# The first stage of element 0 computed by nodes instead of by features

## The chip, the core and the metric

The kernel runs on one core of one Trainium2 chip. The metric is device time in microseconds: 2378.89 us, the median of three runs (2378.59 to 2378.9). All data are float32. TensorE is written PE below, VectorE DVE, ScalarE ACT, GpSimd POOL, SyncE SP; SP, ACT and POOL also issue DMAs.

## The reference

Sixteen elements (graphs of 1024 nodes with 128 features, a full 1024 x 1024 adjacency of weights) pass through two blocks, each followed by a residual and a normalization over the features:

```
# block 0 (embeddings = x, both matrices = adj)
degree = adj.sum(-1)[:, :, None]
sum_neighbors = einsum('bid,bij->bjd', x, adj) / degree
x = layernorm(x + relu(concat([x, sum_neighbors], -1) @ W.T + b))

# block 1: four layers on x, with skips of earlier layers' outputs
def layer(nodes, adj, ws, bs, wd, bd, wn, bn, wu, bu):
    src_agg = einsum('bjv,bij->biv', nodes @ ws + bs, l2norm(adj, rows))
    dst_agg = einsum('bjv,bji->biv', nodes @ wd + bd, l2norm(adj, columns))
    return tanh(concat([src_agg, nodes @ wn + bn, dst_agg], 2) @ wu + bu)
x = layernorm(x + four_layers(x))
```

The degree of a node divides all features of its gathered sum, so it may be applied after the product with the second half of W as well as before it. The norms of the rows and the columns of adj need the sums of squares of all its entries.

## The kernel before

The elements are worked one after another. For elements 1 to 15 the whole first block overlaps the last layers of the element before. Element 0 has nothing before it, so its first block is a stretch of its own, written out line by line (L1131 to L1344), and its layer 0 (the branch `if b == 0`) is a "plain layer" with work hung between the products as hooks: the number of a hook is the number of the product ahead of which it runs. Two z products with the own weights come first (steps 0 and 1), then eight d products of half 1 (2 to 9), eight of half 0 (10 to 17), then sixteen z products with the transposed adjacency (18 to 33).

The order of instructions on every engine is the order in which the program writes them (`manual_schedule`); each engine runs its own list in order, and semaphores hold an instruction until its inputs and its buffer are ready. PSUM buffers come from pools that go round: `ps_s`, reached through `small(...)`, has two banks; `ps_t`, reached through `product(...)` without a number, has four. A buffer is taken again when everything that reads its last contents has run. Each DMA takes one of eight completion semaphores in turn and waits for the DMA that had it before.

The first block of element 0, in order:

- SP (and POOL) load the nodes xn and the adjacency a, in four pairs of row blocks (`PAIRS`, the upper half of the nodes first). Then SP loads layer 0's and layer 1's weights and the bias vectors (`load_biases`), layer 2's weights, adjacency row quarter 2, layer 3's weights, quarters 3, 0 and 1 (`load_rows`). The quarters are loaded once more by rows because they are scaled by the inverse row norms and transposed into `at`.
- `to_xT`: PE transposes the nodes, ACT copies them to xT (features by nodes).
- `squares_of`, `gathers_of`: ACT squares each row block with a row sum (L1225), DVE sums degrees (L1231), PE accumulates the gathered sums pa (L1238). POOL adds the blocks of squares (`add_square`, L1228) for the column norms; ACT's square of the last block, `second`, comes late.
- `degree_inverses` and `degree_row`: the reciprocal degrees, one number per node and so one per partition, are turned by PE into rows that repeat over all partitions (`factor_bank`, L361), copied by ACT into dinv (L1258). `scaled` multiplies the gathered sums by them (L1261) into agT.
- `weights_of_x`, `weights_of_agT`: PE multiplies by the two halves of W (L1265, L1268), features by nodes; ACT applies bias and relu (L1269).
- `with_x`: PE transposes the result back to nodes by features (L1276), DVE adds x (L1278).
- `norm_stats` (L491 to L521): batch statistics per block on DVE; POOL raises the variance to -1/2 with one instruction for the half (L518). `norm_write` on DVE or `norm_write_act` on ACT normalizes in place; `to_x1` transposes to x1T.
- Between these, `fold_begin` and `fold_end` turn each layer's weights into products with wu: PE transposes (L207) into banks, copies by ACT (L208), bias products (L211, L213), weight products (L229), copies (L231, L232).

In layer 0: `messages` forms the messages t from x1T (PE L249, DVE L740), four groups with `second_x1`, `factors_and_fold` and `row_factors0` behind the first three. There `row_inverses` spreads the inverse row norms (DVE L403), `gather_inverses` makes rinv, `column_transpose` and `column_reduce` sum the squares by columns (DVE L341, L346), and `scale_rows` scales row quarters by rinv on ACT, eight instructions a quarter (L688). In the plain layer: hook 2 ends the column inverses on POOL (L397), hook 6 makes the rows cinv of them (PE L361 cinvp, ACT L353), hook 3 transposes quarters 2 and 3 on DVE (L696), `columns0` scales the columns of a in place (L436), `destination` multiplies a half of d by cinv (L904), hooks 9 and 12 fold layer 3's weights, with the scalings of quarters 0 and 1 at hooks 9 and 14, `sums0` combines quarters of the matrices for the next layer (L715, L719, L721) and `finish` adds z and leads to the tanh (L907, L1107). The layer after starts with its messages, tile pt from f1T (L249).

Of the kernel before, what the change touches and what calls it, by code (L numbers as in the profile page):

```python
# [8 lines left out]
F32 = mybir.dt.float32  # L9
# [14 lines left out]
def adj_resnorm_kernel(ctx: ExitStack, tc: tile.TileContext, x, adj, w0, b0, layers, out):  # L24
# [1132 lines left out]
    biases_of = [[b0, *layers[0][1::2], *layers[1][1::2]], [*layers[2][1::2], *layers[3][1::2]]]  # L1157
# [3 lines left out]
    bcs = [columns[0][:, 1:5], columns[0][:, 5:], columns[1][:, :4], columns[1][:, 4:]]  # L1161

    def load_biases(i, q, s=slice(None)):
        for k, v in list(enumerate(biases_of[i]))[s]:
            q.dma_start(in_rows[k:k + 1, i * P:(i + 1) * P], v.rearrange("(o p) -> o p", o=1))

# [84 lines left out]
    yT = one.tile([P, N], F32, tag="f23T", name="yT0")  # L1251
    x1n = two.tile([P, NB, D], F32, tag="sq", name="x1n0")
    x1T = one.tile([P, N], F32, tag="xb", name="x1_0_T")
    dinv = one.tile([P, N], F32, tag="acc", name="dinv0")
    pn, pw = {}, {}

    def degree_row(h):
        nc.scalar.copy(nodes(dinv[:, half(h)]), blocks(factor_bank(2, h, inv, f"dinv0_{h}")))  # L1258

    def scaled(h):  # L1260
        nc.vector.tensor_mul(agT[:, half(h)], pa[h], dinv[:, half(h)])  # L1261

    def weights_of_x(h):
        pw[h] = product(f"pw0_0_{h}")
        nc.tensor.matmul(pw[h], w0T[:, 0], xT[:, half(h)], start=True, stop=False)  # L1265

    def weights_of_agT(h):
        nc.tensor.matmul(pw[h], w0T[:, 1], agT[:, half(h)], start=False, stop=True)  # L1268
        nc.scalar.activation(blocks(yT[:, half(h)]), nodes(pw[h]), AF.Relu, bias=b0c)  # L1269

    def with_x(h):

        pt = ps_t.tile([P, BPH, P], F32, tag="pt", name=f"yn0_{h}")
        for q in range(BPH):
            i = h * BPH + q
            nc.tensor.transpose(pt[:, q], yT[:, i * P:(i + 1) * P], ident)  # L1276
        pn[h] = x1n[:, h * BPH:(h + 1) * BPH]
        nc.vector.tensor_add(pn[h], pt, xn[:, h * BPH:(h + 1) * BPH])  # L1278
# [7 lines left out]
    weights_of_x(1)  # L1286
# [9 lines left out]
    degree_row(1)  # L1296
# [3 lines left out]
    add_square(1)  # L1300
# [510 lines left out]
```

## Time and profile before

The profiled execution took 2377.85 us; its span, from the first to the last instruction, is 2375.8 us.

| engine | busy us | share |
|---|---|---|
| PE (matmul) | 2365.3 | 100% |
| PE (weight load, beside it) | 1309.7 | 55% |
| DVE | 2092.3 | 88% |
| ACT | 981.4 | 41% |
| POOL | 282.7 | 12% |

The stretch that the change touches, by the same execution (busy us of each engine, share of the DMA engines):

| us from the start | PE | DVE | ACT | POOL | DMA |
|---|---|---|---|---|---|
| 7 to 18 | 9.22 of 11 | 5.91 | 5.54 | 5.44 | 1.04 |
| 18 to 24 | 5.90 of 6 | 4.17 | 4.19 | 5.48 | 0.62 |
| 24 to 34 | 9.04 of 10 | 6.35 | 6.15 | 4.31 | 0.70 |
| 34 to 48 | 13.89 of 14 | 12.47 | 8.10 | 6.32 | 1.13 |
| 48 to 64 | 16.00 of 16 | 13.58 | 13.79 | 8.06 | 0.90 |
| 64 to 78 | 14.00 of 14 | 13.86 | 0.72 | 1.42 | 0.94 |

How to read it: PE's products are pipelined and the ends of them are modelled, so that a stretch that shows PE as busy throughout can hold small waits. A float32 product of 128 x 512 appears as two passes. In the lists of the timeline a row gives the start, the length, the engine, the line, the operation, the tiles written and read, the number of instructions joined in the row, and in brackets the idle time before it and what ended that. In the chain of waits a row gives the start, the length and what was running. In the list of waits a row gives who waited for whom, the total in us, how many times, and the longest. DMA-issuing instructions on SP show the time that SP took to issue them, not the transfer.

### The profile page before, as it was taken

To read this page: it belongs to the slowest core of one execution; us is meant where nothing else is said; L and a number is where in the kernel's file an instruction comes from. 1 tells how busy PE (TensorE), PEld (TensorE's weight loads), DVE (VectorE), ACT (ScalarE), POOL (GpSimd) and SP (SyncE) were. 2 spreads that over 40 slices of the span, in tenths; PEclk is the share of its full clock that TensorE was granted. 3 is DMA by queue.
4 is the path that set the end of the run, shared out by engine and by line. 5 is a ranking of instruction groups with operands and counts; after the bars stand their busy time and mean duration, and the time that the engine had idled before them with its cause. 6 is when DMAs were issued, how large, how long until landed. Compare 5 with 4: busy or idle time off the path is not lost.

```text
span 2375.8 us, 39260 instructions
## 1 busy us (share of the span) xinstructions
PE 2365.3 (100%) x15259; PEld 1309.7 (55%) x15259; DVE 2092.3 (88%) x2821; ACT 981.4 (41%) x1859; POOL 282.7 (12%) x104
## 2 busy tenths in 40 slices
PE   9999999999999999999999999999999999999998
PEld 5455555555555555555655555555555555555555
DVE  6999998998988989889988889898899998998954
ACT  6425335352443524445243452534425334352322
POOL 5100111101111011111011110111100111101100
PEclk9999999999999999999999999999999999999999
DMA  8536263362624527244273442725426263362410
GB/s 208 127 89 144 57 141 75 80 138 49 159 60 98 116 54 166 51 106 106 64 156 69 104 92 71 153 65 120 87 72 145 58 139 75 78 142 49 100 22 22
DMA packets 363403, 232.03 MB, mean 98 GB/s; under 512 B 150369, under 2 KB 334322, under 8 KB 363218
## 3 DMA queue, kind: packets, MB, share of 16 engines
q1 hardware_dynamic: 360578, 226.18, 42.6%
q0 software_dynamic: 816, 2.49, 0.4%
q8 instruction: 121, 1.98, 0.3%
q10 hardware_dynamic: 1824, 0.85, 0.1%
q14 instruction: 64, 0.52, 0.1%
HBM read 209.59 MB, written 19.84 MB: 97 GB/s over the span
## 4 chain that ended last, share of the span: by engine, by line
PE 99%; DMA 0%; DVE 0%; SPq 0%; issue 0%; ACT 0%; POOLq 0%; POOL 0%; DVEq 0%
PE m L1094 43%; PE z L1094 26%; PE pt L249 9%; PE pt_z L249 5%; PE m_f L624 5%; PE z_f L624 2%; PE pw L249 2%; PE m3s L1094 2%; PE z L913 1%; PE d L913 1%; PE pt_p L249 1%; PE pa L1238 0%; DMA a<-in_adj_dram 0%; PE wm L229 0%; PE wtr L207 0%; PE pw L1268 0%
## 5 line engine op out<-in xcount | busy, mean ns | idle before, releaser
L1094 PE MATMUL m<-a,t 128*64 128x512 f32 x1008 | 426.7, 593 | 0.0
L1094 PE MATMUL m<-at,t 128*64 128x512 f32 x1008 | 420.4, 592 | 0.0
L1094 PE MATMUL m<-T,S 128*64 128x512 f32 (+1 forms) x1040 | 398.6, 572 | 0.0
L1094 PE MATMUL m<-Q,S 128*64 128x512 f32 x880 | 392.3, 592 | 0.0
L484 POOL TENSOR_TENSOR rs<-ve,mhalf 128x32 f32<-128x32 f32 x30 | 192.1, 6403 | 1018.8 <-DVE ve L482 1018.8
L1094 PE MATMUL z<-at,t 128*64 128x512 f32 (+1 forms) x520 | 229.6, 579 | 0.0
L1094 PE MATMUL z<-a,S 128*64 128x512 f32 x504 | 228.3, 592 | 0.0
L1094 PE MATMUL z<-Q,t 128*64 128x512 f32 (+1 forms) x520 | 227.5, 580 | 0.0
L1094 PE MATMUL z<-a,t 128*64 128x512 f32 (+1 forms) x520 | 227.4, 580 | 0.0
L1094 PE MATMUL z<-at,S 128*64 128x512 f32 x504 | 226.6, 592 | 0.0
L1094 PEld LDWEIGHTS m<-Q,S 128*64 128x64 f32 x880 | 119.4, 137 | 187.2 <-issue 186.5
L1094 PEld LDWEIGHTS m<-T,S 128*64 128x64 f32 x1040 | 133.1, 137 | 123.9 <-issue 118.8
L1094 PEld LDWEIGHTS m<-at,t 128*64 128x64 f32 x1008 | 133.5, 137 | 115.0 <-issue 115.0
L1094 PEld LDWEIGHTS m<-a,t 128*64 128x64 f32 x1008 | 131.3, 137 | 98.6 <-issue 93.6
L946 ACT COPY e<-m 64x512 f32<-64x512 f32 x63 | 36.6, 581 | 339.0 <-PE m L1094 338.6
L1094 PE MATMUL z<-T,t 128*64 128x512 f32 (+2 forms) x400 | 173.0, 575 | 0.0
L397 POOL TENSOR_TENSOR inv<-cols,mhalf 128x16 f32<-128x16 f32 (+1 forms) x16 | 50.0, 3124 | 935.3 <-DVE cols L396 935.3
L436 DVE TENSOR_TENSOR a<-a,cinv 128x512 f32<-128x512 f32 x250 | 154.6, 697 | 0.0
L324 ACT ACTIVATE sq<-a 128x1024 f32<-128x1024 f32 x120 | 125.8, 1050 | 33.0 <-DVE acc L331 19.1
L1094 PEld LDWEIGHTS z<-Q,t 128*64 128x64 f32 x520 | 69.6, 137 | 107.2 <-issue 106.8
L249 PEld LDWEIGHTS pt<-wm,f1T 128*64 128x64 f32 x1536 | 111.1, 137 | 27.0 <-issue 14.9
L319 ACT ACTIVATE a<-a 128x1024 f32<-128x1024 f32 x120 | 125.3, 1045 | 0.4
(328 smaller groups left out, 4999.5 us busy)
## 6 DMA issues: line engine op xcount, KB each, us to landing
a<-in_adj_dram SPq DMA_DIRECT2D x120, 512.0 KB
rows<-in_adj_dram SPq DMA_DIRECT2D x480, 64.0 KB
a<-in_adj_dram SPq DMA_DIRECT2D x240, 128.0 KB
wm<-wsave SPq DMA_DIRECT2D x32, 704.0 KB
wm<-wsave SPq DMA_DIRECT2D x31, 320.0 KB
xs<-in_x_dram SPq DMA_DIRECT2D x60, 128.0 KB
cinv<-dr SPq DMA_DIRECT2D x30, 256.0 KB
dinv<-dr SPq DMA_DIRECT2D x30, 256.0 KB
```

What stands on the lines that cost most here:

```text
L249: nc.tensor.matmul(out[s], x[:, s], y, start=start, stop=stop)
L319: nc.scalar.activation(a[:, i, :], a[:, i, :], AF.Copy, accum_out=degree)
L324: nc.scalar.activation(sq, a[:, i, :], AF.Square, accum_out=state["cols"][:, i:i + 1])
L397: nc.gpsimd.tensor_tensor(inv[:, s], cols[:, s], mhalf[:, s], ALU.pow)
L436: engine.tensor_mul(a[:, i, s], a[:, i, s], cinv[:, s])
L484: nc.gpsimd.tensor_tensor(rstd, ve, mhalf[:, :n], ALU.pow)
L624: nc.tensor.matmul(o, x_, y_, start=start, stop=stop)
L913: nc.tensor.matmul(nodes(o) if len(y.shape) == 4 else o, x_, y, start=start, stop=stop)
L946: nc.scalar.copy(e0[high], A[high])
L1094: nc.tensor.matmul(o, x, y_, start=start, stop=stop)
```

## The change

All of it is in element 0.

- The two products with W give nodes by features at once: blocks of xT (and of agT, now the unscaled gathered sums, copied by ACT) are the stationary operand, W the moving one (`into_rows`). The transposes back and the degree rows go. The inverse degree is a scalar of the partition: DVE multiplies the second product by it and adds the first with the bias row b0r (`x_and_bias`, `with_degrees`); relu and the residual are one instruction (`with_x`). b0r is loaded by a DMA that repeats b0 over the partitions.
- The statistics are done by pairs of blocks (`two_stats`), each with a power of its own on POOL.
- The squares of the last two row blocks are made earlier, and two additions of squares go to DVE; one of POOL's goes away.
- Biases are loaded in three groups: of layers 0 and 1 on SP ahead of layer 1's weights, of layer 2 on ACT's queue, of layer 3 on SP behind row quarter 2.
- The spread of the row inverses and rinv come ahead of the messages; two of quarter 2's scalings come into `second_x1`. Quarters 0 and 1 are scaled at hooks 8 and 9, ahead of layer 3's fold (hooks 13 and 16), and transposed at hook 12. POOL takes four of the column scalings of half 0 in place of six.

The diff, cut to its core:

```diff
-    biases_of = [[b0, *layers[0][1::2], *layers[1][1::2]], [*layers[2][1::2], *layers[3][1::2]]]
+    biases_of = [[b0, *layers[0][1::2], *layers[1][1::2]], layers[2][1::2], layers[3][1::2]]
+    b0r = one.tile([P, N], F32, tag="acc", name="b0r")[:, :P]
-        nc.scalar.copy(nodes(xT[:, half(h)]), blocks(pt))
+        nc.scalar.copy(xT[:, half(h)], pt)
     for l, q in enumerate((None, None, 2, 3)):
-        if l in (1, 2):
-            load_biases(l - 1, nc.sync)
+        if l == 3:
+            load_biases(2, nc.sync)
         fetched.append(fetch_weights(raw, l, nc.sync, bcs[l], None if l else wm))
+        if l == 0:
+            nc.sync.dma_start(b0r, b0.rearrange("(o p) -> o p", o=1).to_broadcast([P, P]))
+            load_biases(0, nc.sync)
...
+    def into_rows(name, xs, k, h):
+        pw[k, h] = ps_t.tile([P, BPH, P], F32, tag="pt", name=f"{name}_{h}")
         for q in range(BPH):
             i = h * BPH + q
-            nc.tensor.transpose(pt[:, q], yT[:, i * P:(i + 1) * P], ident)
+            nc.tensor.matmul(pw[k, h][:, q], xs[:, i * P:(i + 1) * P], w0T[:, k], start=True, stop=True)
+    def gathered(h):
+        nc.scalar.copy(blocks(agT[:, half(h)]), nodes(pa[h]))
+    def x_and_bias(h):
+        nc.vector.tensor_add(xw[:, rows_of(h)], pw[0, h], b0r[:, None, :].to_broadcast([P, BPH, P]))
+    def with_degrees(h, qs):
+        for q in qs:
+            i = h * BPH + q
+            nc.vector.scalar_tensor_tensor(xw[:, i], pw[1, h][:, q], inv[:, 2 * NB + i:2 * NB + i + 1], xw[:, i],
+                                           op0=ALU.mult, op1=ALU.add)
+    def with_x(h):
+        s = rows_of(h)
+        nc.vector.scalar_tensor_tensor(x1n[:, s], xw[:, s], 0.0, xn[:, s], op0=ALU.max, op1=ALU.add)
+    def two_stats(h, first, shifted=False):
...
+        for q in (first, first + 1):
+            nc.vector.bn_stats(stats[:, q], x1n[:, h * BPH + q])
+            nc.vector.bn_aggr(mv[:, q], stats[:, q])
+        nc.vector.tensor_scalar_add(ve[:, s], mv[:, s, 1], LN_EPS)
...
+        nc.gpsimd.tensor_tensor(rstd[:, s], ve[:, s], mhalf[:, s], ALU.pow)
...
-    weights_of_x(1)
+    into_rows("px", xT, 0, 1)
...
     degree_inverses(1)
-    degree_row(1)
     squares_of(*PAIRS[2])
     gathers_of(*PAIRS[2])
     add_square(0)
-    add_square(1)
...
     gather(1, second)
+    square(first)
+    degree_inverses(0)
+    x_and_bias(1)
+    gathered(1)
+    into_rows("px", xT, 0, 0)
+    into_rows("pg", agT, 1, 1)
+    square(second)
+    load_biases(1, nc.scalar)
+    nc.vector.tensor_add(sq[1], sq[1], sq[first])
+    add_square(1)
+    x_and_bias(0)
+    gather(0, first)
     bias_columns(0)
-    degree_inverses(0)
-    degree_row(0)
-    scaled(1)
-    weights_of_agT(1)
-    gather(0, first)
-    square(first)
     gather(0, second)
-    add_square(first)
-    scaled(0)
+    gathered(0)
+    with_degrees(1, range(BPH))
     with_x(1)
-    weights_of_x(0)
-    weights_of_agT(0)
-    stats = {1: norm_stats(pn[1], range(BPH), "0_0_1", True)}
-    fold_begin(0, fetched[0])
-    with_x(0)
+    two_stats(1, 0, True)
+    biases = fold_begin(0, fetched[0], later=True)
+    into_rows("pg", agT, 1, 0)
+    two_stats(1, 2)
+    root_inverses(cols, inv, slice(NB))
+    biases()
     fold_end(0, fetched[0])
-    square(second)
-    other_half = norm_stats(pn[0], range(2), "0_0_0", then=True)
-    for q in range(2, BPH):
-        norm_write(pn[1][:, q], pn[1][:, q], stats[1], q)
-    stats[0] = other_half(range(2, BPH))
-    root_inverses(cols, inv, slice(NB))
-    add_square(second)
-    biases = fold_begin(1, fetched[1], nc.vector.tensor_copy, True)
-    for q in range(2):
-        norm_write_act(pn[1][:, q], pn[1][:, q], stats[1], q)
+    with_degrees(0, range(2))
+    written(1, 0, norm_write_act)
+    biases = fold_begin(1, fetched[1], later=True)
+    for q in range(1, BPH):
+        written(1, q)
+    with_degrees(0, range(2, BPH))
+    spread = row_inverses(0, inv)
     to_x1(1)
     biases()
     fold_end(1, fetched[1])
+    with_x(0)
+    two_stats(0, 0)
+    rinv = gather_inverses(0, spread)
+    two_stats(0, 2)
     for q in range(BPH):
-        norm_write(pn[0][:, q], pn[0][:, q], stats[0], q)
+        written(0, q)
...
             def row_factors0():
-                for q in (2, 3):
-                    scale_rows(rows[q], q, rinv)
+                scale_rows(rows[2], 2, rinv, range(2, QB))
+                scale_rows(rows[3], 3, rinv)
             def second_x1():
                 bias_columns(1)
                 fold_begin(2, fetched[2])
-                ahead["spread"] = row_inverses(0, inv)
+                scale_rows(rows[2], 2, rinv, range(2))
+                nc.vector.tensor_add(sq[4], sq[4], sq[second])
                 ahead["tr"] = column_transpose(0, st0)
...
             hooks = {0: weights0, 2: lambda *_: inverses(0, st0, NB), 3: rows0, 6: cinv0,
-                     9: lambda *_: fold_and_scale(3, 0), 11: second0, 12: folded(3, fold_end),
-                     14: lambda *_: scale_rows(rows[1], 1, rinv), 18: first0, 26: sums0}
+                     8: lambda *_: scale_rows(rows[0], 0, rinv), 9: lambda *_: scale_rows(rows[1], 1, rinv),
+                     11: second0, 12: first_rows, 13: fold_last, 16: lambda *_: fold_end(3, fetched[3]),
+                     14: lambda *_: columns0(range(NJ, NB), 0, nc.gpsimd), 18: first0, 26: sums0}
```

`fold_last` is `bias_columns(2)` and `fold_begin(3, ...)`; `first_rows` transposes quarters 0 and 1 and scales the columns 0 to 3 of half 1; `second0` keeps the scaling of columns 4 to 7 of half 1 and `destination(1)`; `first0` is `destination(0)` and DVE's scaling of columns 0 to 3 of half 0.

More of the change, by code (lines that the diff above doesn't have):

```diff
@@ L1160, in adj_resnorm_kernel, with load_biases @@
     columns = [raw.take(len(v)) for v in biases_of]
-    bcs = [columns[0][:, 1:5], columns[0][:, 5:], columns[1][:, :4], columns[1][:, 4:]]
-    def load_biases(i, q, s=slice(None)):
-        for k, v in list(enumerate(biases_of[i]))[s]:
+    bcs = [columns[0][:, 1:5], columns[0][:, 5:], columns[1], columns[2]]
+    def load_biases(i, q):
+        for k, v in enumerate(biases_of[i]):
             q.dma_start(in_rows[k:k + 1, i * P:(i + 1) * P], v.rearrange("(o p) -> o p", o=1))
+    b0r = one.tile([P, N], F32, tag="acc", name="b0r")[:, :P]
     def bias_columns(i):
@@ L1250, in adj_resnorm_kernel @@
     agT = one.tile([P, N], F32, tag="f1T", name="agT0")
-    yT = one.tile([P, N], F32, tag="f23T", name="yT0")
+    xw = one.tile([P, NB, D], F32, tag="f23T", name="xw0")
     x1n = two.tile([P, NB, D], F32, tag="sq", name="x1n0")
     x1T = one.tile([P, N], F32, tag="xb", name="x1_0_T")
[L1254 to L1273, printed above, removed]
+    pw, of_half = {}, {}
+    def rows_of(h):
+        return slice(h * BPH, (h + 1) * BPH)
@@ L1274, in with_x @@
+    def into_rows(name, xs, k, h):
+        pw[k, h] = ps_t.tile([P, BPH, P], F32, tag="pt", name=f"{name}_{h}")
         for q in range(BPH):
             i = h * BPH + q
-            nc.tensor.transpose(pt[:, q], yT[:, i * P:(i + 1) * P], ident)
-        pn[h] = x1n[:, h * BPH:(h + 1) * BPH]
-        nc.vector.tensor_add(pn[h], pt, xn[:, h * BPH:(h + 1) * BPH])
+            nc.tensor.matmul(pw[k, h][:, q], xs[:, i * P:(i + 1) * P], w0T[:, k], start=True, stop=True)
+    def gathered(h):
+        nc.scalar.copy(blocks(agT[:, half(h)]), nodes(pa[h]))
@@ new lines, in two_stats @@
+    def two_stats(h, first, shifted=False):
+        if h not in of_half:
+            of_half[h] = (one.tile([P, BPH, 6], F32, tag="stats", name=f"st0_0_{h}"), [
+                two.tile([P, BPH, n] if n > 1 else [P, BPH], F32, tag=tag, name=f"{tag}0_0_{h}")
+                for tag, n in (("mv", 2), ("ve", 1), ("rst", 1), ("shift", 1))])
+        stats, (mv, ve, rstd, shift) = of_half[h]
+        s = slice(first, first + 2)
+        for q in (first, first + 1):
+            nc.vector.bn_stats(stats[:, q], x1n[:, h * BPH + q])
+            nc.vector.bn_aggr(mv[:, q], stats[:, q])
+        nc.vector.tensor_scalar_add(ve[:, s], mv[:, s, 1], LN_EPS)
+        if shifted:
+            nc.vector.tensor_scalar_mul(shift[:, s], mv[:, s, 0], -1.0)
+        nc.gpsimd.tensor_tensor(rstd[:, s], ve[:, s], mhalf[:, s], ALU.pow)
+        if shifted:
+            nc.gpsimd.tensor_mul(shift[:, s], shift[:, s], rstd[:, s])
@@ L1280, in to_x1, with written @@
+    def written(h, q, write=norm_write):
+        mv, _, rstd, shift = of_half[h][1]
+        v = x1n[:, h * BPH + q]
+        write(v, v, (mv, rstd, shift), q)
     def to_x1(h):
@@ L1345, in adj_resnorm_kernel @@
     at = [transposed(0, h) for h in range(NH)]
-    back = rinv = None
+    back = None
     for b in range(B):
@@ L1366, in second_x1 @@
                 fold_begin(2, fetched[2])
-                ahead["spread"] = row_inverses(0, inv)
+                scale_rows(rows[2], 2, rinv, range(2))
+                nc.vector.tensor_add(sq[4], sq[4], sq[second])
                 ahead["tr"] = column_transpose(0, st0)
             def factors_and_fold():
-                nonlocal rinv
                 to_x1(0)
@@ L1374, in factors_and_fold @@
                 column_reduce(0, st0, ahead["tr"])
-                rinv = gather_inverses(0, ahead["spread"])
             ahead = {}
@@ L1398, in second0, with first_rows, fold_last, first0 @@
                 destination(1, cinv[0])
-                columns0(range(NJ), 1)
-            def fold_and_scale(l, q):
-                fold_begin(l, fetched[l])
-                scale_rows(rows[q], q, rinv)
-            def first0(destination, finish):
-                columns0(range(NJ, NB), 0, nc.gpsimd)
-                columns0(range(2), 0, nc.gpsimd)
+            def first_rows(destination, finish):
                 for q in (0, 1):
                     transpose_rows(rows[q], q, at)
+                columns0(range(NJ), 1)
+            def fold_last(destination, finish):
+                bias_columns(2)
+                fold_begin(3, fetched[3])
+            def first0(destination, finish):
                 destination(0, cinv[0])
-                columns0(range(2, NJ), 0)
+                columns0(range(NJ), 0)
             def sums0(destination, finish):
@@ L1418, in sums0 @@
                 combine(3, y, T)
-            def folded(l, part):
-                return lambda *_: part(l, fetched[l])
             hooks = {0: weights0, 2: lambda *_: inverses(0, st0, NB), 3: rows0, 6: cinv0,
-                     9: lambda *_: fold_and_scale(3, 0), 11: second0, 12: folded(3, fold_end),
-                     14: lambda *_: scale_rows(rows[1], 1, rinv), 18: first0, 26: sums0}
+                     8: lambda *_: scale_rows(rows[0], 0, rinv), 9: lambda *_: scale_rows(rows[1], 1, rinv),
+                     11: second0, 12: first_rows, 13: fold_last, 16: lambda *_: fold_end(3, fetched[3]),
+                     14: lambda *_: columns0(range(NJ, NB), 0, nc.gpsimd), 18: first0, 26: sums0}
             T = combined(0, "T")
```

## The prediction

> **What bounds the kernel now.** I read the page first: TensorE is busy the whole span. The stretch from 84 to 2370 us, in the second fence (start and end, length, then busy TensorE, weight loads, VectorE, ScalarE, GpSimd, clock, DMA), leaves it 0.35 us idle.
>
> ```profile
> span 2375.8 us, 39260 instructions
> PE 2365.3 (100%) x15259; PEld 1309.7 (55%) x15259; DVE 2092.3 (88%) x2821; ACT 981.4 (41%) x1859; POOL 282.7 (12%) x104
> ```
>
> ```profile
> 84.00:2370.00 2286.00, 2285.65 (x14930) 1267.44 (x14926) 2027.80 (x2716) 934.96 (x1752) 244.79 (x64) 1.00 0.42 93
> ```
>
> The change lies in the first 80 us. As later work leaves TensorE no gap, the forecast is the shift of the moment when TensorE enters layer 1 of element 0 (its first pt at 77.28 us), added to the time. The chain of waits up to 90 us, next, says what holds that moment:
>
> ```profile
> 4.01 9.36 DMA a<-in_adj_dram
> 13.51 3.67 PE pa L1238 x8
> 17.62 0.44 PE dinv L361 x4
> 18.15 5.39 PE pa L1238 x12
> 27.16 0.44 PE yn L1276 x4
> 30.79 0.70 DVE x1n L1278
> 34.01 0.47 DVE raw L208
> 48.74 0.87 PE cinvp L361 x8
> 63.62 13.73 PE z L913 x32
> 77.35 3.80 PE pt L249 x32
> ```
>
> The adjacency loads hold it to 18 us, VectorE from 30.79 to 34.5, TensorE itself otherwise. So up to 18 us nothing is to be won; after it there are 1.7 us of transposes and some 3.7 us of VectorE's stretch. Then the timelines of ScalarE, SP and GpSimd, and the waits, show who is just in time for TensorE:
>
> ```profile
> 48.04 3.30 ACT L688 ACTIVATE Q<-Q,rinv 128x256 f32<-128x256 f32 x8 [2.67 <-DMA Q<-in_adj_dram]
> 51.25 1.04 ACT L353 COPY cinv<-cinvp 128x512 f32<-128x512 f32 x2
> 52.56 1.25 ACT L208 COPY raw<-wtr 128x384 f32<-128x384 f32 x3 [0.27 <-PE wtr L207]
> 54.24 3.29 ACT L688 ACTIVATE Q<-Q,rinv 128x256 f32<-128x256 f32 x8
> 58.93 3.31 ACT L688 ACTIVATE rows<-rows,rinv 128x256 f32<-128x256 f32 x8
> ```
> ```profile
> 26.81 0.40 SPq L191 DMA_DIRECT2D raw<-in_L_gnn_ws_dram  x1
> 53.05 0.40 SPq L681 DMA_DIRECT2D rows<-in_adj_dram  x1
> ```
> ```profile
> 46.63 1.65 POOL L397 TENSOR_TENSOR inv<-cols,mhalf 128x8 f32<-128x8 f32 x1 [7.67 <-DVE cols L396]
> ```
> ```profile
> PEld wtr L207 <- ACT cinv L353: 0.5, 1, 0.5
> ```
>
> ScalarE copies layer 3's transposed weights (52.56) between the row scalings; quarter 3's scaling waited for its load until 48.04. The last line matters most: layer 3's transposes already wait for ScalarE to empty a PSUM bank of the two-bank pool.
>
> **The change part by part.** Instructions run in the written order on each engine.
>
> *TensorE, first stage.* Two groups of four dinv transposes and two of yn go: 16 x 0.107 = 1.7 us. The four 128x512 products (0.86 each, 3.4) become 16 of 128x128 in two passes of 0.107 (3.4): zero. One more bias transpose: +0.15.
>
> *VectorE.* Gone: two agT multiplies (0.69 each), two additions of x (0.68), a fold copy (0.55). New: two additions of the bias row and two max-and-add (0.69 each by the 128x512 rows), two additions of squares (1.2 each, as at 15.76), and eight 128x128 scalar-times-tensor-plus-tensor, which the trace does not show: 0.21 (successive 128x128 additions, 44.59 to 44.80) to 0.34 (L525's mean); I take 0.28, the spacing of the four L525 in 1.11 us. The sum is +4.0 us of VectorE, beside TensorE. GpSimd loses one addition of 2.36 us; VectorE's 128x32 L403 took 1.88 us beside it, against 0.18 for the like L389, so 1.7 comes back. Powers by pairs: 128x4 took 1.05, 128x8 1.63, hence 0.7 to 1.05 per pair; four pairs add 0.8 to 2.1 us on GpSimd; the first comes two blocks earlier. The degree no longer gates the gathered sums; it comes in by the scalar, after the product.
>
> *ScalarE's DMAs.* Four bias loads move from SP to ScalarE, behind square(second) (ending about 25.4): 4 x 0.44 (the ACTq pair at 123.43 took 0.87), plus waits, since each load waits for the one that used its semaphore before, here up to layer 2's third weight, issued near 25.6. I take release at 28.7 (about 3 us after issue); ends 27.2 (no wait) and 31. Behind it stand the bias columns, agT's second half and the fold copies; TensorE waits for them at bm0 and pg_0. I get pg_0 done at 30.6 and layer 0's products at 31.2, where before they began their last at about 31.2: even. Even at 31 the later slack covers it.
>
> *To x1.* First half: the gathered sums end at 23.5 as before; copy 0.65, pg_1 0.86: 25.2. VectorE: 4 x 0.28, then max-and-add 0.69, held to 26.8 by GpSimd's addition (24.45 to 26.8): 27.5; two blocks of statistics 0.8, two small 0.2; power and shift end by 29.8. ScalarE writes block 0 after layer 0's copies, at 32.4: transposes near 32.5 (before 33.48). Second half: pg_0 at 30.6; 4 x 0.28, three writes, spread (after the row inverses on GpSimd, about 32) 0.2, max-and-add, statistics 1.9, last power, writes: 36.6, transposes at 36.7 (38.94).
>
> *To the column inverses.* x1T's second copy stands behind two scalings of quarter 2 (landed by 38.6 before, when SP issued the load eight places on): TensorE's last messages end at 41.8. VectorE does, from 36.6: message add 0.65, the added squares 1.2, transpose 1.2, add 0.6, reduction 1.15, two adds (0.65 each), nine weight sums (2.3, 43.61 to 45.92), own, reduction and max 0.65, GpSimd's 1.65. With 0.2 of hand-overs, that is 47.5 for cinvp, against 48.58; ends 47.0 and 49.0. The TensorE gain of some 3 us at the first messages is thus cut to 1.1 here.
>
> *SP and the row loads.* Before layer 2's weights SP loses eight bias loads (24.37 to 26.81, 2.4 us) and gains the broadcast of b0 (0.35, by the weights' rows): weights and rows start 2.1 us earlier. DMA was nearly idle from 26 to 28 (share 0.05) and full after (1.21 from 32 to 43, 0.90 to 53); layer 1's weights now come straight before, so I take 1.8. Against it: each load waits for the eighth before it, and small loads now hold four places. Ends: 2.2 earlier, 1.0 later. Quarter 0's last piece had landed by 53.05, where SP issued the load eight places behind; so 51.2, between 50.8 and 54.0.
>
> *Layer 3's fold: the new wait.* Before, fold_begin(3) preceded the scaling of quarters 0 and 1 on ScalarE. Now hooks 8 and 9 put both scalings ahead, and hook 13 adds bias_columns(2) to the two-bank pool: biases2, then the first transposes, then the second group in the bank of biases2. That group needs ScalarE's copy of biases2, which is queued behind 16 scalings.
> - TensorE gets there at 47.5 + 0.87 + 7 x 0.86 + 0.15 + 0.35 = 54.9.
> - ScalarE: quarter 0 lands 51.2; 3.3 + 3.3 + 0.2 = 58.0. (Its own earliest, without loads: quarter 3 at 46.2, + 3.3 + 1.04 + 6.8 = 57.3.)
> - Stall 3.1 us. The rest by the old rows (52.03 to 77.28 = 25.25, less four d products now ahead, 3.43, and one transpose group, 0.33) is 21.5: the z products end at 79.5, 2.2 later. Before, pt lost 0.25 to finish(0) (3.68 for 3.42 of passes); VectorE now has time, so +2.0.
>
> Who waits behind TensorE: layer 3's saved weights go out some 4 us later, so element 1's adjacency load (65.22) starts about 2 us later; its reader at 79.06 shifts by as much. VectorE's transposes and column scaling end near 64, before z needs them at 72.
>
> [...] The rows: the first passes after launch take 0.84 us (L1185, six in 5.03), later ones 0.43; a pause of 1.05 us before 13.51 cost nothing after it (eight passes in 3.67, against 3.63). So a pause of 3.1 costs between nothing and 6 x 0.41 = 2.5 more; I take nothing, the pause being nearest. [...]
>
> **The rivals.**
> 1. *No wait at the fold* (rows land much earlier, or ScalarE is ahead). For it: ScalarE idles 2.67 us at 48.04. Then 54.9 + 21.5 = 76.4, 0.9 ahead, and the 0.25: -1.1, 2377.8; if the inverses also come sooner, up to the 3 us gained earlier, 2375.9.
> 2. *Slower than the bound.* Row loads with fewer in flight: quarter 0 lands not at 51.2 but after 54.0. Then ScalarE is free at 60.8 and the shift is 4.8: 2383.7 and more. It decides from 54.0 on. For it: SP waited for the eighth load 17 times already; against: the share of 1.21 and 0.90 leaves the DMA engines little idle to lose.
> 3. *Faster by over 0.2%.* All 1.7 us of transposes and all 3.7 us of VectorE's stretch, nothing behind: -5.4, 2373.5. Against: the inverses, and ScalarE's floor of 57.3.
>
> **How the numbers follow.** The profiled execution took 2377.85 us (2.05 outside its span), 1.04 below the median 2378.89, to which I add: 2378.89 + 2.0 = 2380.9. Chances: this 0.60, rival 1 0.19, rival 2 0.17, rival 3 0.04. 0.2% (4.8 us) is about what a measurement of this kernel can tell from no change: faster 0.04, same 0.79, slower 0.17. The range leaves out the far parts of rivals 2 and 3: 2377.0 to 2384.3. The likeliest case alone: 2379.9 (floor 57.3 and a later arrival) to 2382.5.
>
> **What would show it.** Right: TensorE idle 2 to 4 us between 54 and 59 before wtr of layer 3, released by ScalarE's L1173; L688 running without a break for 6.6 us before it; cinvp near 47.5; no dinv or yn; L403 near 0.2 us; z ending near 79.5; after that the same trace. Wrong: rows landing at 53 or later, passes of 0.84 us after the pause, a TensorE gap before 45 us behind ScalarE's DMA issues, or a gap after 80 us.

## The result, and the profile after

The changed kernel took 2386.18 us (median of 8, 2382.26 to 2386.89) against 2378.89 us of the kernel before (8 runs on the same chip, 2378.59 to 2379.73): ratio 1.0028, 95% interval 1.0018 to 1.0039, slower by 7.3 us. The forecast was 2380.9 us in a range of 2377.0 to 2384.3, with 0.17 on slower by over 0.2%. The profiled execution took 2386.21 us, 8.36 us more than that of before. The page, and the long stretch that answers to 84 to 2370 us of before:

```profile
span 2384.4 us, 39278 instructions
PE 2366.9 (99%) x15268; PEld 1145.7 (48%) x15268; DVE 2094.1 (88%) x2835; ACT 981.1 (41%) x1858; POOL 273.7 (11%) x102
```
```profile
84.00:2380.00 2296.00, 2294.20 (x14979) 1105.07 (x14977) 2035.53 (x2730) 942.00 (x1763) 245.01 (x66) 1.00 0.43 94
```

TensorE again has hardly a gap after 84 us. Layer 1's first sums (m, L1094) start at 91.08 us, against 82.70 before: 8.4 us, which is the whole loss. TensorE's timeline up to there (start, length, what, and in brackets the idle time before the row and what ended it):

```profile
18.95 5.39 PE L1243 MATMUL pa<-a,xn 128*128 128x512 f32 x12 [0.61 <-issue]
...
30.43 0.71 PE L211 MATMUL bm<-raw 128*128 128x128 f32 x4 [1.85 <-ACT b0c L1175]
...
34.25 0.63 PE L1313 MATMUL x1tr<-ident,x1n 128*128 128x128 f32 x4
...
49.50 1.09 PE L361 MATMUL cinvp<-ident,inv 128*128 128x128 f32 x8 [0.19 <-POOL inv L397]
50.43 6.17 PE L913 MATMUL d<-a,t 128*128 128x512 f32 x14
56.53 0.22 PE L1172 MATMUL biases<-ident,biases 4*128 4x4 f32 x1
56.68 0.55 PE L207 MATMUL wtr<-ident,raw 128*128 128x128 f32 x3
61.46 1.54 PE L207 MATMUL wtr<-ident,raw 128*128 128x128 f32 x6 [4.23 <-ACT raw L1173]
62.80 1.06 PE L211 MATMUL bm<-raw 128*128 128x128 f32 x4
...
63.94 4.53 PE L913 MATMUL d<-a,t 128*128 128x512 f32 x6
68.31 2.17 PE L229 MATMUL wm<-raw 128*128 128x128 f32 x18
...
72.03 13.90 PE L913 MATMUL z<-at,t 128*128 128x512 f32 x32
85.86 3.67 PE L249 MATMUL pt<-wm,f1T 128*64 128x256 f32 x32
...
91.08 0.59 PE L1094 MATMUL m<-a,t 128*64 128x512 f32 x1
```

The same places in the kernel before:

```profile
18.15 5.39 PE L1238 MATMUL pa<-a,xn 128*128 128x512 f32 x12
...
48.58 1.04 PE L361 MATMUL cinvp<-ident,inv 128*128 128x128 f32 x8
...
52.03 1.19 PE L207 MATMUL wtr<-ident,raw 128*128 128x128 f32 x9
...
53.64 2.82 PE L913 MATMUL d<-a,t 128*128 128x512 f32 x6
...
82.70 0.59 PE L1094 MATMUL m<-a,t 128*64 128x512 f32 x1
```

The first line of each is the twelve gathered-sum products that follow the third pair of adjacency blocks. They start at 18.95 us, 0.8 us later than before (18.15). The delay is there ahead of anything new: GpSimd issues the second of its last four adjacency loads at 9.36 us, before at 8.09, while the first load that the change adds, that of b0r, is issued at 15.54; and further executions put the start of the twelve anywhere up to 20.70. So I count from this start, in the text "from the start of the twelve". By that count the column inverses (cinvp) are reached at 30.55 us (before 30.43), and m at 72.13 us (before 64.55): 7.58 us lost, 7.46 of them between the two.

The row at 61.46 is the wait that the prediction foresaw, for ScalarE's copy of the third bias group (L1173), with 4.23 us instead of 3.1. The rows behind it show what it did not foresee: six transposes and four bias products in 1.54 and 1.06 us, six d passes (three products) in 4.53 us; runs further down show the same rows in 0.88, 0.61 and 2.82 us. The stretches around it, with the granted clock in the third column from the end:

```profile
57.20:60.56 3.36, 0.03 (x1) 0.00 (x0) 0.61 (x1) 2.49 (x7) 1.55 (x2) 1.00 0.69 200
60.56:63.97 3.41, 2.51 (x13) 2.51 (x13) 2.57 (x3) 2.19 (x7) 0.00 (x0) 0.50 0.51 211
63.97:67.38 3.41, 3.41 (x5) 1.46 (x6) 2.18 (x4) 0.54 (x2) 1.31 (x2) 0.50 0.00 0
67.38:70.80 3.42, 3.42 (x23) 2.63 (x22) 0.00 (x0) 1.37 (x6) 0.00 (x1) 1.00 0.00 0
```

TensorE's clock is halved from 60.56 to 67.38 us, 6.8 us long; of that, 5.9 us lie behind the pause and do half of their work, which costs some 3 us. Why ScalarE came so late is in its own timeline and in the list of waits (who waited for whom, total, times, longest):

```profile
50.19 1.08 ACT L353 COPY cinv<-cinvp 128x512 f32<-128x512 f32 x2
52.10 3.30 ACT L688 ACTIVATE Q<-Q,rinv 128x256 f32<-128x256 f32 x8 [0.84 <-DMA rows<-in_adj_dram]
58.07 3.30 ACT L688 ACTIVATE rows<-rows,rinv 128x256 f32<-128x256 f32 x8 [2.66 <-DMA kept<-x1n]
61.27 0.14 ACT L1173 COPY raw<-biases 128x4 f32<-128x4 f32 x1
61.31 0.47 ACT L208 COPY raw<-wtr 128x384 f32<-128x384 f32 x1
```
```profile
PE wtr L207 <- ACT raw L1173: 4.2, 1, 4.2
...
ACT rows L688 <- DMA kept<-x1n: 2.7, 1, 2.7
...
ACT raw L1173 <- DMA raw<-in_L_gnn_wn_dram: 4.1, 1, 4.1
```

Quarter 0 is scaled from 52.10, quarter 1 only from 58.07, after 2.66 us of idleness behind a transfer. (The transfer named, a write of x1n, is one that SP issued later than quarter 1's loads; what the scaling needs is the load.) The last line is the other new wait: ScalarE held by its own four bias loads, and behind it TensorE for 1.85 us at 30.43.

### The profile page after: what moved, and what is told of

It is laid out like the page before. It is cut to its first block, busy times and chain, and to the rows that moved or that the text cites. A ratio compares the mean times of both kernels' runs of the same rounds, so it can differ in the third digit from the quotient of the medians.

```text
span 2384.4 us, 39278 instructions
## 1 busy us (share of the span) xinstructions
PE 2366.9 (99%) x15268; PEld 1145.7 (48%) x15268; DVE 2094.1 (88%) x2835; ACT 981.1 (41%) x1858; POOL 273.7 (11%) x102
## 4 chain that ended last, share of the span: by engine, by line
PE 97%; DMA 2%; SPq 0%; DVE 0%; ACT 0%; issue 0%; POOLq 0%; POOL 0%; DVEq 0%
PE m L1094 44%; PE z L1094 24%; PE pt L249 9%; PE pt_z L249 5%; PE m_f L624 5%; PE m3s L1094 2%; PE z_f L624 2%; PE pw L249 2%; DMA Q<-in_adj_dram 1%; PE pt_p L249 1%; PE z L913 1%; DMA wm<-in_L_gnn_ws_dram 1%; PE d L913 0%; DMA a<-in_adj_dram 0%; SPq L681 0%; DMA kept<-x1n 0%
## 5 line engine op out<-in xcount | busy, mean ns | idle before, releaser
L1094 PE MATMUL m<-a,t 128*64 128x512 f32 x1008 | 425.1, 593 | 0.0
L1094 PE MATMUL m<-at,t 128*64 128x512 f32 x1008 | 420.4, 592 | 0.0
L1094 PE MATMUL m<-T,S 128*64 128x512 f32 (+1 forms) x1040 | 398.5, 572 | 0.0
L1094 PE MATMUL m<-Q,S 128*64 128x512 f32 x880 | 392.3, 592 | 0.0
L1094 PE MATMUL z<-at,t 128*64 128x512 f32 (+1 forms) x520 | 229.6, 579 | 0.0
L1094 PE MATMUL z<-a,S 128*64 128x512 f32 x504 | 228.3, 592 | 0.0
L1094 PE MATMUL z<-Q,t 128*64 128x512 f32 (+1 forms) x520 | 227.5, 580 | 0.0
L1094 PE MATMUL z<-a,t 128*64 128x512 f32 (+1 forms) x520 | 227.4, 580 | 0.0
L1094 PE MATMUL z<-at,S 128*64 128x512 f32 x504 | 226.6, 592 | 0.0
L1094 PEld LDWEIGHTS m<-Q,S 128*64 128x64 f32 x880 | 119.4, 137 | 215.7 <-issue 213.9
L1094 PEld LDWEIGHTS m<-T,S 128*64 128x64 f32 x1040 | 128.7, 137 | 141.5 <-issue 136.4
L1094 PEld LDWEIGHTS m<-at,t 128*64 128x64 f32 x1008 | 131.3, 137 | 131.9 <-issue 131.9
L1094 PEld LDWEIGHTS m<-a,t 128*64 128x64 f32 x1008 | 129.7, 137 | 114.5 <-issue 107.3
L1094 PE MATMUL z<-T,t 128*64 128x512 f32 (+2 forms) x400 | 173.0, 575 | 0.0
L1094 PEld LDWEIGHTS z<-Q,t 128*64 128x64 f32 x520 | 69.6, 137 | 123.1 <-issue 122.4
L249 PE MATMUL pt<-wm,f1T 128*64 128x128 f32 (+1 forms) x1536 | 120.5, 308 | 0.0
```

Of the source, the lines that this page charges most:

```text
L249: nc.tensor.matmul(out[s], x[:, s], y, start=start, stop=stop)
L1094: nc.tensor.matmul(o, x, y_, start=start, stop=stop)
```

## The experiments

Theory: of the 7.6 us, the order of ScalarE's work at layer 3's fold costs most, as a wait of 4.2 us plus some 3 us of passes at half clock; the wait is as long as it is because quarter 1's load lands late. Rivals: the new first stage itself costs it, or the bias loads on ScalarE's queue, or the slow passes have another cause.

All times are medians, beside the kernel before on the same chip (2378.99 for the first four, 2379.08 for the next four, 2379.19 for the last four). "To m" is the profiled execution's first m less the start of the twelve. Where the text sets two runs of different groups against each other, it takes their medians as they are; the kernel before, beside them, differs by up to 0.3 us from group to group. In the lines of e4, e7 and e11 the numbers of the source lines are shifted by the lines that the run adds: four in e4 and e7, two in e11.

| run | us | against before | interval of the ratio | to m |
|---|---|---|---|---|
| before | 2378.89 | | | 64.55 |
| changed | 2386.18 | +7.3 | 1.0018 to 1.0039 | 72.13 |
| e1 old order | 2380.92 | +1.9 | 0.9997 to 1.0014 | 66.45 |
| e2 before, new order | 2381.43 | +2.4 | 1.0000 to 1.0018 | 66.77 |
| e3 quarter 1 later | 2384.15 | +5.2 | 1.0012 to 1.0030 | 67.62 |
| e4 warm | 2383.78 | +4.8 | 1.0013 to 1.0031 | 68.74 |
| e5 biases on SP | 2386.86 | +7.8 | 1.0020 to 1.0045 | 72.38 |
| e6 old order, biases on SP | 2379.22 | +0.1 | 0.9993 to 1.0011 | 64.72 |
| e7 old order, warm | 2380.32 | +1.2 | 0.9997 to 1.0014 | 67.83 |
| e8 third group early | 2380.94 | +1.9 | 0.9998 to 1.0015 | 66.68 |
| e9 each group ahead | 2378.22 | -1.0 | 0.9987 to 1.0005 | 63.80 |
| e10 quarter 2 behind | 2378.64 | -0.6 | 0.9988 to 1.0006 | 63.30 |
| e11 fewer bytes | 2380.77 | +1.6 | 1.0000 to 1.0017 | 66.57 |
| e12 sum on GpSimd | 2380.22 | +1.0 | 0.9995 to 1.0012 | 65.71 |

### e1: the old order of the scalings

```diff
+            def fold_last():
                 bias_columns(2)
                 fold_begin(3, fetched[3])
+                scale_rows(rows[0], 0, rinv)
...
-                     8: lambda *_: scale_rows(rows[0], 0, rinv), 9: lambda *_: scale_rows(rows[1], 1, rinv),
-                     11: second0, 12: first_rows, 13: fold_last, 16: lambda *_: fold_end(3, fetched[3]),
-                     14: lambda *_: columns0(range(NJ, NB), 0, nc.gpsimd), 18: first0, 26: sums0}
+                     9: lambda *_: fold_last(), 11: second0, 12: lambda *_: fold_end(3, fetched[3]),
+                     14: lambda *_: scale_rows(rows[1], 1, rinv), 18: first0, 26: sums0}
```

(`second0` and `first0` are again those of the kernel before.)

> The changed kernel with the end of layer 0 in the old order: before layer 3's fold ScalarE has no scaling of quarters 0 and 1; quarter 0 is scaled behind the fold's first part, quarter 1 two products further on, the transposes as before. The new first stage, the pairs and the bias loads stay. Theory (wait at layer 3's fold plus a cold TensorE after it cost 7 of the 8.4 us by which layer 1 starts later): no pause over 1 us near 55 to 62 us, every d product after the fold at 0.43 us a pass; layer 1's first m at 83.0 to 84.0 instead of 91.1, what stays being the 0.9 us by which the column inverses come later; 2378.5 to 2380.5. Rival (the first stage by nodes, its pairs of statistics or ScalarE's four bias loads cost it): still 2384 or more, with the loss seen before 54 us.

2380.92 us: 5.3 of the 7.3 us are gone; that is 0.4 us above the theory's range. The fold now runs without a wait (last row of TensorE's timeline below). What is left is further ahead: the 1.87 us pause behind ScalarE's bias loads, and slow rows after it (0.71 and 1.14 us in the changed kernel's profile).

```profile
30.99 1.22 PE L211 MATMUL bm<-raw 128*128 128x128 f32 x4 [1.87 <-ACT b0c L1175]
...
32.29 2.06 PE L1269 MATMUL pg<-w0T,agT 128*128 128x128 f32 x8
...
55.46 1.20 PE L207 MATMUL wtr<-ident,raw 128*128 128x128 f32 x9
```
```profile
27.60:31.00 3.40, 1.53 (x7) 0.74 (x7) 3.16 (x13) 0.29 (x3) 1.63 (x2) 1.00 0.80 228
31.00:34.40 3.40, 3.40 (x16) 3.40 (x17) 0.41 (x4) 1.35 (x4) 2.57 (x4) 0.50 0.69 174
```

Half clock for 3.4 us after 1.87 us of idleness, where the changed kernel's 1.85 us at the same place left the clock at 1.00. Its runs fall in two groups, three at 2378.3 to 2379.4 and eight at 2380.6 to 2381.3; that the groups are these two cases is argued, since only one execution is profiled.

### e2: the kernel before with the new order

The hooks and the functions `first_rows` and `first0` of the change, on the kernel before; the biases stay in two groups.

> The kernel before with the new order of the end of layer 0 alone: both scalings ahead of layer 3's fold, transposes of both quarters ahead of the first half's columns, the fold's second part at the sixteenth product. No third bias group, so both of the two-bank pool's banks are free when the fold's transposes come; the second part must wait for ScalarE's copies instead, which end 1.9 us after the scalings. [...] Rival (the first stage is what costs): 2378.9 within 1 us.

2381.43 us, in the range forecast for the order alone (2380.4 to 2386): it costs 2.4 us without any part of the new first stage. As expected it is the fold's second part that waits, for ScalarE's copies of the transposed weights:

```profile
64.59 2.27 PE L229 MATMUL wm<-raw 128*128 128x128 f32 x18 [2.00 <-ACT raw L208]
```

The clock stayed at 1.00 (62 to 68 us). The twelve started at 20.70 us here, 2.55 us later than in the profiled execution of before, with the same instructions ahead of them: that much is chance.

### e8: the third bias group early

```diff
                 cinv[0] = factor_rows_now(0, 1, inv, "cinv")
+                bias_columns(2)
...
-                bias_columns(2)
                 fold_begin(3, fetched[3])
```

> The changed kernel with the third bias group's transpose and copy moved ahead of the two scalings (behind the column inverses), nothing else. Theory: the fold's transposes then find both banks free and run at their arrival, near 56.7 us; TensorE does 2.6 us of d products before its second part, which must wait for ScalarE's copies of the transposed weights (scalings to 61.3, copies to 62.5): a wait of 1 to 2 us instead of 4.2, too short for slow passes; layer 1's first m at 84.5 to 86; 2380 to 2382. Rival (any TensorE wait behind the scalings costs the same, wherever it stands): 2385 or more.

2380.94 us. One ScalarE copy of under 0.2 us, moved ahead of the scalings with the TensorE transpose that feeds it, takes back 5.2 of the 7.3 us. No wait is left at the fold:

```profile
59.62 1.15 PE L207 MATMUL wtr<-ident,raw 128*128 128x128 f32 x9
...
63.85 2.17 PE L229 MATMUL wm<-raw 128*128 128x128 f32 x18
```

I had expected 1 to 2 us at the second row; in this execution TensorE came later, because the first pause (2.12 us here) was followed by 3.4 us at half clock. That waits of 1 to 2 us are too short for slow passes is not shown: the clock stayed at 1.00 after the changed kernel's 1.85 us and went to 0.50 after e1's 1.87. So it matters where TensorE is held: held ahead of the transposes, it cannot use the transposes, the bias products and six d passes (4.2 us in these rows) to cover ScalarE's scalings; held behind them, it can.

### e4: the price of the clock

```diff
+    WARM = 18
...
             pt = small(name, [BPH, P]) if c < 2 else product(name).rearrange("p (k v) -> p k v", v=P)
+            for _ in range(WARM if l == 3 and c == 0 else 0):
+                nc.tensor.matmul(pt[:, 3], ident, ident, start=True, stop=True)
```

> The changed kernel with 18 products of the identity with itself (128x128, 0.214 us each in this stage: 3.9 us) on TensorE just ahead of layer 3's first transposes, into the unused fourth column block of their bank. They fill the wait of 4.2 us with work that no one reads; the wait itself stays. Theory (after the pause the passes run at half speed for some 7 us, which costs 2.9 us): six transposes of the fold in 0.8 instead of 1.54 us, the six d products after it in 2.7 instead of 4.5; layer 1's first m at 88.0 to 88.8 instead of 91.1; 2383.0 to 2384.0. Rival (the slow passes have another cause, a wait for operands or for banks): no change, 2386.

2383.78 us, 2.4 us faster than the changed kernel with 18 products more, and 3.4 us earlier at m in the profiled executions. TensorE's timeline:

```profile
60.67 1.18 PE L211 MATMUL wtr<-ident,raw 128*128 128x128 f32 x9
61.68 0.61 PE L215 MATMUL bm<-raw 128*128 128x128 f32 x4
...
62.27 2.82 PE L917 MATMUL d<-a,t 128*128 128x512 f32 x6
```

ScalarE is as late as before (its copy at 60.78), and the d passes after it take 2.82 instead of 4.53 us. So the slow rows are the clock, and with TensorE busy through the wait the clock stays up: 1.00 from 53.7 to 70.8 us here, 0.50 from 60.56 to 67.38 us in the changed kernel. Part of the 3.4 us, some 0.5, is that ScalarE was that much earlier in this execution.

### e3: quarter 1's scaling behind the fold

`scale_rows(rows[1], 1, rinv)` and quarter 1's transposes move behind `fold_end(3)` at hook 16; quarter 0 stays at hook 8.

> The changed kernel with quarter 1's scaling and its transposes moved behind the second part of layer 3's fold; quarter 0 stays ahead. ScalarE is then free at 52.1 + 3.3 = 55.4 us, before TensorE comes to the fold at 56.7. Theory: the wait of 4.2 us goes and with it the slow passes, quarter 1 is scaled by 63 to 65 us and transposed by 68, before z needs it at 66 to 75: layer 1's first m at 83.5 to 85.5; 2378.5 to 2381. Rival (first stage): 2384 or more. A loss between the two would say that quarter 1 is then late for z.

2384.15 us, a miss. The wait at the fold is gone, but a new one stands at the entry to layer 1. TensorE, then VectorE, in the profiled execution:

```profile
83.08 1.95 PE L249 MATMUL pt<-wm,f1T 128*64 128x256 f32 x16 [2.88 <-ACT f1T L1107]
```
```profile
66.66 2.37 DVE L696 STREAM_TRANSPOSE at<-rows 128x1024 f32<-128x1024 f32 x2 [4.22 <-ACT rows L688]
...
81.58 0.68 DVE L907 TENSOR_TENSOR e<-e,z 128x512 f32<-128x512 f32 x1
```

I had asked only whether quarter 1 is in time for z. It is; but VectorE waits 4.22 us for it in its own order, and its combinations then push `finish(0)` to 81.58, 62.6 us from the start of the twelve and 3.1 us later than before (77.72, or 59.6 by that count). This profiled execution, at 2381.72 us, was the fastest of eleven; what the others lost beyond it no trace shows.

### e5: the bias loads on SP

```diff
-        if l == 3:
-            load_biases(2, nc.sync)
+        if l == 2:
+            load_biases(1, nc.sync)
+            load_biases(2, nc.sync)
...
-    load_biases(1, nc.scalar)
```

> The changed kernel with all eight bias loads of layers 2 and 3 on SP ahead of layer 2's weights, as in the kernel before; none on ScalarE's queue. The order of the scalings stays new. Theory (wait at layer 3's fold, held by quarter 1's load, plus cold passes): TensorE's 1.85 us pause near 28.5 to 30.4 us goes, but the fold still waits for ScalarE: quarter 1's load decides that. If SP's eight loads in flight, four of them small bias loads, are what left the DMA queues at 0.5 to 0.8 from 30 to 38 us, quarter 1 lands 1 to 2 us earlier counted from the last adjacency load, and the wait is 2 to 3.5 us instead of 4.2; if the bytes alone set it, it lands as late and the wait grows by what TensorE gains. 2382 to 2386. Rival (the bias loads on ScalarE's queue are the cost): 2379 to 2380.

2386.86 us: neither is it the cost of ScalarE's queue (2379 to 2380), nor was there anything to win by more loads in flight. The pause at 30 us is gone and TensorE reaches the inverses 0.6 us sooner, but the wait at the fold is 5.79 us. ScalarE:

```profile
54.70 3.30 ACT L688 ACTIVATE Q<-Q,rinv 128x256 f32<-128x256 f32 x8 [1.26 <-DMA rows<-in_adj_dram]
59.45 3.30 ACT L688 ACTIVATE rows<-rows,rinv 128x256 f32<-128x256 f32 x8 [1.44 <-DMA wsave<-wm]
```

SP began quarter 2 at 31.55 us (27.57 in the changed kernel), 3.5 us later by the count from the start of the twelve, and quarter 1 landed 40.05 us after that start instead of 39.12: most of a late issue is made up, the DMA engines being at a share of 1.2 from 38 us on.

### e11: fewer bytes ahead of quarter 1

Without the loads of layer 3's weights ws, wd and wn; the place is zeroed at the start.

> The changed kernel without the loads of layer 3's three first weights (590 KB; their place is zeroed once by VectorE at the start, so layer 3 computes with zeros there). Nothing else is moved. Theory (quarter 1's landing, 39.1 us after the last adjacency load's first product, is set by the bytes ahead of it: the queues move some 200 KB a us and are full from 42 to 56 us): quarters 0 and 1 land 2.5 to 3 us earlier, so ScalarE comes to the fold's copy some 2.8 us earlier; TensorE waits 1 to 2 us instead of 4.2, with no or one half-speed stretch of 3.4 us instead of two: 2379.5 to 2382. Rival (number of loads in flight or SP's issue decides, not bytes): quarter 1 at 38.5 to 39.5 us, 2385 to 2387.

2380.77 us, as the theory has it. Quarter 1 is scaled straight behind quarter 0 (ScalarE, then TensorE):

```profile
52.75 3.31 ACT L690 ACTIVATE Q<-Q,rinv 128x256 f32<-128x256 f32 x8
55.95 3.30 ACT L690 ACTIVATE rows<-rows,rinv 128x256 f32<-128x256 f32 x8
```
```profile
59.35 0.88 PE L209 MATMUL wtr<-ident,raw 128*128 128x128 f32 x6 [0.52 <-ACT raw L1175]
```

It had landed by 36.4 us after the start of the twelve, at least 2.7 us earlier; the wait is 0.52 us and the six transposes run at full speed. (Some 1.0 us of the shorter wait is not the load's: TensorE came to the inverses at 31.59 us from the start of the twelve instead of 30.55, behind the 1.63 us pause and 3.4 us at half clock.) The three issues of the loads went too (some 1.5 us of SP), so bytes and issues are not fully apart here; e5, where quarter 2's issue 3.5 us later made quarter 1 land 0.9 us later, speaks for the bytes. So does the spacing: wherever ScalarE stood waiting for both quarters, the second was scaled 5.97 (changed), 5.28 (e2), 5.35 (e4) and 4.75 us (e5) after the first, and 8 loads of 128 KB at the 200 GB/s that the trace shows there take 5.2 us.

### e6, e7: what the old order leaves

e6 is e1 with the loads of e5; e7 is e1 with 8 products as in e4, ahead of layer 0's fold.

> The new first stage with the old order of the scalings and with the bias loads on SP. Theory: what was left over the kernel before when only the order was put back (2380.9 against 2379.0) is the 1.87 us pause of TensorE behind ScalarE's bias loads, and above all the slow passes that followed it in the profiled run (four products in 1.22 instead of 0.71 us, eight in 2.06 instead of 1.14, clock 0.5 from 32 to 34 us). Without that pause: no clock below 1.0, 2377.8 to 2379.0, as the kernel before or up to 1 us faster. Rival (VectorE's longer first stage is what is left): still 2380 to 2381, with a wait of TensorE for the column inverses of 0.5 us or more.

> The new first stage with the old order of the scalings, bias loads on ScalarE's queue as changed, and 8 products of the identity with itself (0.107 a pass, 1.7 us) ahead of layer 0's fold, into the unused column block of its bank: they fill the 1.87 us pause and shorten nothing. Theory (slow passes after that pause cost 1.7 to 2.3 us in most runs; the runs without the products fell in two groups, 2378.3 to 2379.4 and 2380.5 to 2381.3): all runs in the lower group, median 2378.3 to 2379.4. Rival (the two groups come from the time at which the adjacency loads land): two groups again, median 2380.5 to 2381.

e6: 2379.22 us, 1.7 us faster than e1, with no stretch below full clock from 26 to 60 us; 0.2 us above the theory's range, as TensorE now waits 1.62 us for the second copy of x1T, behind quarter 2's late load in ScalarE's order. (The trace names an addition of VectorE as what released those scalings, which they do not read; in e9 below, where SP begins quarter 2 at 29.74 us instead of 31.49, the wait is gone.) So the pause and its slow passes are what e1 lacked, not VectorE's longer stage. e7: 2380.32 us, a miss that tells little: in its profiled execution ScalarE was released only at 31.84 us, so the pause followed the products that should have filled it, and 3.4 us at half clock came again:

```profile
32.12 0.71 PE L215 MATMUL bm<-raw 128*128 128x128 f32 x4 [1.82 <-ACT b0c L1179]
```

That execution took 2381.67 us, the second slowest of the eleven; why the other nine below it, at 2379.8 to 2380.7, are not in e1's lower group no trace shows.

### e9, e10, e12: towards a better kernel

e9 is e1 with four bias loads on SP ahead of layer 2's weights and four ahead of layer 3's. e10 is e9 with all of quarter 2's scalings behind x1T's copy, as before the change. e12 is e10 with the last sum of squares back on GpSimd, behind the row inverses.

> The new first stage, the old order of the scalings, and each group of bias loads on SP just ahead of its layer's weights (four ahead of layer 2's, four ahead of layer 3's), none on ScalarE's queue. When all eight stood ahead of layer 2's, the row loads began 4 us later and TensorE waited 1.6 us at its third messages for x1T's copy, which stood behind two scalings of quarter 2. Theory: with four, SP is 1.2 to 1.5 us later than in the changed kernel, quarter 2 is there in time and that wait falls to under 0.5 us; no pause near 29 us, clock 1.0 throughout; TensorE's entry into layer 1 64.0 to 64.7 us after the last adjacency load's first product (before: 64.55); 2378.3 to 2379.3. Rival (VectorE's chain to the column inverses is then the bound): TensorE waits 1 us or more for them, and the time stays at 2379.2 or above.

> The same with quarter 2's first two scalings back behind x1T's second copy, as in the kernel before, so that no copy that TensorE needs stands behind a row load. Theory: no wait of TensorE before the third messages whatever the landing; where the load was in time already, no difference: 2378.0 to 2379.3, within 0.3 us of the kernel with the two ahead. Rival (ScalarE's order there matters): 0.5 us or more apart.

> The kernel with quarter 2's scalings behind and each bias group ahead of its weights, and the last sum of squares back on GpSimd behind the row inverses, as in the kernel before. It takes 1.2 us from VectorE ahead of the column inverses and gives GpSimd 2.4 us there. Theory (VectorE's chain to the inverses has at most 0.2 us of slack at TensorE's arrival, so that the freed TensorE waits for it): the wait for the inverses shrinks by up to 1 us: 2377.3 to 2378.8. Rival (GpSimd's addition then holds the powers of the second half's pairs, or slows VectorE beside it): the same time or up to 2 us more.

e9 takes 2378.22 us and e10 2378.64, both just under the 2379.19 of the kernel before beside them, by less than can be told from no change (e9 0.1 us below its range); their executions reach m 0.75 and 1.25 us sooner. The rival of e9 shows in part, a wait of 0.88 us for the inverses:

```profile
49.05 1.09 PE L361 MATMUL cinvp<-ident,inv 128*128 128x128 f32 x8 [0.88 <-POOL inv L397]
```

e12 is 1.6 us slower than e10, as its rival says: beside GpSimd's addition (32.80 to 35.14) VectorE's small spread takes 2.33 us instead of 0.18, and TensorE pauses 1.92 us for it, with 3.4 us at half clock after the pause.

```profile
32.87 2.33 DVE L403 TENSOR_TENSOR sp<-inv,group 128x32 f32<-128x32 f32 x1 [0.40 <-POOL inv L397]
```

So the first stage by nodes with the sum on VectorE may be worth up to 1 us, which these runs do not resolve; the new order and ScalarE's loads lose more than that.

## Why the prediction was wrong

The direction and the place were right: the time goes to a wait of TensorE for L1173 at layer 3's fold. The prediction said +2.0 us, the medians differ by 7.3. By its steps, its times less 18.15 and those of after less 18.95:

- *Up to 18 us nothing is won.* Right. The 0.8 us by which the twelve start later is within what executions differ (18.15 to 20.70 us), and the profiled execution of before has the earliest start of the fourteen; that the 1.04 us added to come to the median answers to that is argued, not shown.
- *VectorE and GpSimd.* Right: the four scalar-times-tensor instructions took 1.13 us (predicted 4 x 0.28), the powers 0.70 to 0.72 (the lower end), L403 0.18.
- *ScalarE's DMAs: "even".* Wrong by 1.2 us. Release at 30.15 us, or 29.35 in the clock of before, where 28.7 was taken and 31 allowed; TensorE lost 1.85 us there. The 3 us from issue to landing were an estimate for which the prediction names no row; layer 2's third weight was issued at 26.55 us, and the fourth bias load, held by it, at 29.88, 3.3 us later. The slack that was to cover even 31 was not there. The inverses were to come at 29.35 us from the start of the twelve and came at 30.55. Without these loads (e9) they came at 29.24: the rest of that sum was right.
- *Quarter 0 at 51.2.* Right: 33.05 predicted, 33.15 measured. SP's earlier start did what was said.
- *ScalarE free at 51.2 + 3.3 + 3.3 + 0.2.* This step failed. It has the scaling of quarter 1 follow that of quarter 0 at once, and no term for quarter 1's own megabyte, which was scaled 4.75 to 5.97 us behind quarter 0's in the four runs above, with the DMA engines at a share of 1.2; it was there at 39.1 where 36.4 was needed. ScalarE came 2.6 us late (42.5 instead of 39.9).
- *Stall 3.1.* 4.23: 2.6 more by ScalarE, 1.5 less because TensorE came later (38.3 instead of 36.8).
- *"A pause of 3.1 costs between nothing and 2.5 more; I take nothing."* This step failed as well. The rest was to take 21.5 us and took 24.4; the 2.9 us are the half clock, 0.50 from 60.56 to 67.38 us. The nearest row, a pause of 1.05 us, was the wrong one to lean on: pauses of 1.63 to 2.12 us were followed by half clock in five executions. Slow passes after the pause were among the prediction's own signs of being wrong, as was the gap behind ScalarE's DMA issues.
- *The 0.25 us at pt, and nothing after.* Right: pt took 3.67 us in one row without a wait, and the loss at m is the loss of the time.

2.0 + 2.6 + 2.9 = 7.5, against 7.58 in the profiled executions; the inverses' 1.2 us lie inside the wait, which ScalarE ends. Of the rivals, number 2 came nearest in its time, but not by its mechanism: it had quarter 0 land after 54.0.

## What to carry to other kernels

If several loads feed work that stands in one engine's order, give each its own landing, its bytes over the rate at which the queues run there (here some 200 GB/s, 5.2 us a quarter), and not only the first. A copy that frees a bank of a small pool belongs ahead of work that waits for a load (e8: one 0.2 us copy moved, 5.2 us). Price a TensorE pause with the half-speed stretch that may follow it: here one of 3.4 us came after five pauses of 1.63 to 2.12 us, and none after six of 1.55 to 2.00 and one of 2.88 us; at a clock of 0.50 each such stretch does 1.7 us less work.

## What was not expected of the hardware

- Half clock (0.50) came, between 20 and 90 us, in stretches of 3.4 us: one after the pauses of 1.63 (e11), 1.82 (e7), 1.87 (e1), 1.92 (e12) and 2.12 us (e8), two after 4.23 (changed) and 5.79 us (e5); none after 1.55 (e5), 1.56 (e3), 1.62 (e6), 1.69 (e4), 1.85 (changed), 2.00 (e2) and 2.88 us (e3). Length alone does not decide. What sorts these executions is TensorE's work in windows of 3.41 us, the length of one stretch. In eight of them (the changed kernel, e1, e5, e7, e8, e11, e12, and e9, which has a stretch from 11.22 us on) the start of half clock fixes a grid of such windows. From 7.8 us (e11 and e12: from 18) to 84 us, the eight full-clock windows that TensorE worked for at most 1.78 us were each followed by half clock (0.08 in the changed kernel, 1.54 in e1, 1.78 in e11). The others held at least 1.85 us (e5's 40.09 to 43.50, with the 1.55 us pause), and none was. The changed kernel's 1.85 us pause is cut by a border at 29.84, so that its two windows hold 2.15 and 2.82 us. A window at half clock with 2.51 us of work (60.56 to 63.97) or 1.13 us (e5) was followed by a second one; those with 3.24 us and more were not. That is a reading of these traces after the fact; no run was made for it, and e2, e3, e4 and e6 have no grid here on which to place their pauses.
- The adjacency loads, the same in all kernels, let the twelve products start between 18.15 and 20.70 us: 2.5 us of a single execution's time, as much as most of the effects compared here.
